# Two attention layers on one core: when the output weights are asked for, and where four key chains lie

## The chip, the cores and the metric

The kernel runs on one core of a Trainium2 chip. Times are microseconds (us) on the device, from launch to end, and lower is better. The kernel before was measured three times: 2955.73 us in the median, 2946.95 the lowest and 2957.67 the highest. A profile of one further execution shows each instruction on each engine: TensorE (PE in the profile, its weight loads PEld), VectorE (DVE), ScalarE (ACT), GpSimd (POOL), and SP, whose queue issues nearly all transfers.

## The reference

Four batches of 1024 tokens pass through two layers of cross-attention, all in float32. The context has 1024 tokens of 384 features. Layer 0 has 16 heads of 64, layer 1 has 16 heads of 32 with rotated, normalised queries and keys.

```python
# layer 0
h = layernorm(x) * gamma + beta
Q, K, V = h @ Wq, ctx @ Wk, ctx @ Wv            # 16 heads of 64
vals = (softmax(Q K^T) * 64**-0.5) @ V
x = x + vals @ Wo + bo
# layer 1
xn = x * rsqrt(mean(x * x) + eps) * norm_w
q, k, v = xn @ wq, split(ctx @ wkv)             # 16 heads of 32
q, k = rotate(q), rotate(k)                     # rotary tables cos, sin
q, k = q / max(|q|, eps), k / max(|k|, eps)
x = x + (softmax(q k^T * sqrt(32)) @ v) @ wout
```

## The kernel before, in words

**Tiles.** A batch's x is held as eight tiles of 128 tokens x 512 features. Layer 0 is worked through in eight pairs of heads (p = 0 to 7; a pair is 128 of the 1024 inner features). For each pair there are eight steps (i = 0 to 7), one for each 128 query tokens. Layer 1 follows in two halves of eight heads each.

**A step of layer 0** (`Attention0.step`). TensorE makes the scores s of both heads (line 365); VectorE takes the row maximum m (390); ScalarE computes exp into e (391); GpSimd scales e by the reciprocal of its sum (396); in the next step VectorE transposes e in blocks of 32 (399). The scores stand in two PSUM tiles, so the next step's scores wait until exp has read them. After every second step `regroup` issues sixteen transfers of 128 KB on SP (line 410), which bring the transposed blocks of e, two steps together, into place as eT: this is called a block, four in a pair. `product` (line 426) multiplies eT with the values into av; it runs in odd steps, and takes the block that is the older of two, about three steps after its regroup was asked for.

**Units.** All other work of TensorE (projections of later pairs, sums of outputs, the beginning of layer 1) is cut into units with a cost in us, and stands in a queue, `Units`. After its scores, each step takes as many units from the queue as `fill(us)` allows; `us` is all work that is still to do in layer 0, divided by the steps left. `later` is the planner's account of work that is not yet in the queue, `left` that of the values which join it at step 4 of pair 7. `made` marks how far the queue must be emptied before a pair ends. The order on every engine is the order in which the program is written out by these loops: VectorE, ScalarE, GpSimd and SP work through their instructions strictly in it.

**Output sums** (`add_units`, matmuls recorded at line 163 with the name po). For two pairs of heads together, eight sums of two units each (0.86) multiply their values with 256 rows of Wo and VectorE adds the result into a tile of x (line 293). Sums for pairs 0 and 1 stand in pairs 2 and 3, four in each; those for 2 and 3 in pairs 4 and 5; those for 4 and 5 in pairs 6 and 7; those for 6 and 7 after pair 7. `wo_load` (line 643) asks for the 256 rows, 512 KB, on SP; there are two buffers for them, shared with layer 1's output weights. The first three loads of a batch are written at the start of pairs 2, 4 and 6, the fourth at that of pair 7. In the second to fourth batch, the sums of the last half of layer 1 of the batch before (`tail`) lie in pairs 0 and 1, and the finished tiles are stored from there.

**Key chains** (`rotated_chains`). The keys of layer 1's first half are made in pairs 6 and 7, in four chains of 256 tokens. A chain has a projection (six units of 0.44, named k_p), which ends in a rotation: ScalarE squares the bank (476), VectorE multiplies it with cos and sin, adds, and sums the squares (478 to 483), GpSimd makes the norm's inverse and multiplies (485 to 489). Later its turn-over (one unit of 0.45, k_t, line 499) transposes it on TensorE and ScalarE copies it out (504). The values of the same half are four value chains of six units of 0.44 in pair 7. The wk half that the chains read is overwritten by the one for the second half, `reload`.

**Banks.** Four PSUM banks, f0 to f3, are handed out in turn by `bank` to projections, sums, turn-overs and av. A bank's next user waits until its last one has been copied or added out. While `which["from"]` is 0, which is in layer 0, a key chain's bank is remembered in `which["kept"]` and passed over each time round, until that chain's turn-over; the dictionary `kept` tells whose it is. In layer 1 three banks, f1 to f3, go round.

Of the kernel before, what the change touches and what calls it, by code (L numbers as in the profile page):

```python
# [46 lines left out]
NPAIR = INNER // P  # L47
# [61 lines left out]
def xattn_kernel(ctx: ExitStack, tc: tile.TileContext, a: dict, out: bass.AP):  # L109
    nc = tc.nc  # L110
    x, c = a["x"], a["ctx_768"]
# [12 lines left out]
    which = {"n": 0, "from": 0, "cols": 2, "kept": None}  # L124

    def bank(name):

        while True:
            which["n"] = which["n"] + 1 if which["n"] < 3 else which["from"]
            if which["n"] != which["kept"]:  # L130
                break
        return ps_f.tile([P, 512], F32, tag=f"f{which['n']}", name=name)

    def evac(dst, src):
# [315 lines left out]
    def rotated_chains(dst, src, nk, w, name, tmp):  # L450

        hd, nh = HD1 // 2, TH * FH // HD1
        tiles, kept = {}, {}

        def heads(ap):
            return ap.rearrange("p (t h d) -> p t h d", t=TH, d=HD1)

        def spread(ap):
            return ap.unsqueeze(2).to_broadcast([P, TH, FH // HD1, ap.shape[2]])

        def project(t0, i, k):
            if i == 0 and k == 0:
                tiles[t0] = [bank(f"{name}_p{t0}")]
                if which["from"] == 0:
                    which["kept"] = kept[t0] = which["n"]
            pp = tiles[t0][0]
            t = t0 + i
            lhsT = src[t // 4][:, k, (t % 4) * P : (t % 4 + 1) * P]
            matmul(pp[:, i * FH : (i + 1) * FH], lhsT, w(k), k == 0, k == nk - 1)
            if i == TH - 1 and k == nk - 1:  # L470
                rotate(t0, pp)

        def rotate(t0, pp):

            t1, t2, sq = tmp.take()
            nc.scalar.activation(sq, pp, AF.Square)
            c_, s_ = cos[:, t0 : t0 + TH, :], sin[:, t0 : t0 + TH, :]
            nc.vector.tensor_mul(heads(t1), heads(pp), spread(c_))
            nc.vector.tensor_mul(heads(t2)[:, :, :, :hd], heads(pp)[:, :, :, hd:], spread(s_[:, :, :hd]))
            nc.vector.tensor_mul(heads(t2)[:, :, :, hd:], heads(pp)[:, :, :, :hd], spread(s_[:, :, hd:]))  # L480
            nc.vector.tensor_add(t1, t1, t2)
            ss = sb.tile([P, nh], F32, tag="ss", bufs=2, name=f"{name}_s{t0}")
            nc.vector.tensor_reduce(ss, sq.rearrange("p (h d) -> p h d", d=HD1), AX.X, ALU.add)
            sm = sb.tile([P, nh], F32, tag="sm", bufs=2, name=f"{name}_m{t0}")
            nc.gpsimd.tensor_scalar_max(sm, ss, EPS_L2 * EPS_L2)
            ri = sb.tile([P, nh], F32, tag="ri", bufs=2, name=f"{name}_r{t0}")
            rsqrt(ri, sm)
            t1h = t1.rearrange("p (h d) -> p h d", d=HD1)
            nc.gpsimd.tensor_mul(t1h, t1h, ri.unsqueeze(2).to_broadcast([P, nh, HD1]))
            tiles[t0] = t1  # L490

        def turn_over(t0):
            t1 = tiles.pop(t0)
            if which["kept"] == kept.get(t0):
                which["kept"] = None
            pt = bank(f"{name}_t{t0}")
            for g in range(2):
                for i in range(TH):
                    nc.tensor.transpose(
                        pt[:, (g * TH + i) * P : (g * TH + i + 1) * P],  # L500
                        t1[:, i * FH + g * P : i * FH + (g + 1) * P],
                        ident,
                    )
            nc.scalar.copy(dst()[:, :, t0 * P : (t0 + TH) * P], pt.rearrange("p (g t) -> p g t", g=2))  # L504

        return [
            (
                [(0.44, lambda t0=t0, i=i, k=k: project(t0, i, k)) for i in range(TH) for k in range(nk)],
                [],
                [(0.45, lambda t0=t0: turn_over(t0))],  # L510
            )
            for t0 in range(0, NT, TH)
        ]
# [127 lines left out]
    def wo_load(src, i, name):  # L641
        w = sb.tile([P, 2, DQ], F32, tag="wo", bufs=2, name=name)
        nc.sync.dma_start(w, src[i * 2 * P : (i + 1) * 2 * P, :].rearrange("(n p) m -> p n m", p=P))
        return w

    def flat(lists):
        return [u for lst in lists for u in lst]
# [68 lines left out]
    for b in range(B):  # L716
# [3 lines left out]
        wo = {}  # L720
# [3 lines left out]
        for p in range(NPAIR):  # L724
            if p == 4:
                wk, wv = half_kv_load(0, 0), half_kv_load(0, 1)

            later = costs["pair"] * max(5 - p, 0) + costs["out"] * (7 - p - (b == 0 and p == 0))
            later += costs["k"] * (p < 6) + costs["v"] * (p < 7)
            other = []  # L730
            if p < 2:
                other = tail[p * len(tail) // 2 : (p + 1) * len(tail) // 2]
            elif p % 2 == 0:
                i = p // 2 - 1
                wo[i] = wo_load(a["Wo"], i, f"wo0_{b}_{i}")
                outs = add_units(
                    xt,
                    lambda n: pairs[n]["vals"],
                    lambda n, i=i: wo[i][:, n % 2, :],
                    f"po0_{b}_{i}",  # L740
                    (p - 2, p - 1),
                )
                other = flat(outs[:4])
            else:
                other = flat(outs[4:])
            if p == 6:
                kq = {}

                def begin(n, kq=kq, b=b):
                    kq[n] = qk_tile(f"{n}1_{b}_0")  # L750

                k = rotated_chains(lambda kq=kq: kq["k"], ct, NC_, lambda k, wk=wk: wk[:, k, :], f"k1_{b}_0", RowScratch())
                other = [(0.0, lambda: begin("k"))] + k[0][0] + outs[0] + k[1][0] + outs[1] + k[0][2] + outs[2] + k[2][0] + k[1][2] + outs[3]
            if p == NPAIR - 1:
                last = outs[4:]
                wo[3] = wo_load(a["Wo"], 3, f"wo0_{b}_3")
                outs = add_units(
                    xt, lambda n: pairs[n]["vals"], lambda n: wo[3][:, n % 2, :], f"po0_{b}_3", (6, 7)
                )
                xnT = []  # L760
                norms = norm_units(b, 1, xnT, lambda h: xt[4 * h : 4 * h + 4])
                v = []

                def begin_v():
                    v.extend(sb.tile([P, NT, P], F32, tag="v", bufs=3, name=f"v1_{b}_0_{g}") for g in range(2))

                vs = value_chains(v, wv, ct, f"pv1_{b}_0")
                wk1 = []
                reload = [(0.0, lambda wk1=wk1: wk1.append(half_kv_load(1, 0)))]
                other = last[0] + k[3][0] + reload + last[1] + k[2][2] + last[2] + last[3] + k[3][2]  # L770
                values = [(0.0, begin_v)] + flat(c[0] for c in vs)
            ahead = st["project"](p + 2) if p + 2 < NPAIR else []
            n = 7 * (p == 0)
            work.add(ahead[:n] + other)
            if p % 2 or other and p == 0:
                made[p + 1] = work.end()
            work.add(ahead[n:])
            if p + 2 < NPAIR:
                made[p + 2] = work.end()
            if p == 5:  # L780
                wq = []
                work.add([(0.0, lambda wq=wq: wq.append(half_q_load(0)))])
            left = costs["v"] if p == NPAIR - 1 else 0.0
            for i in range(NT):
                if b == 0 and p == 0 and i == 3:
                    work.until(begun)
                if left and i == 4:
                    work.add(values)
                    left = 0.0
                if 1 <= p <= 2 and i % 2 == 0:  # L790
                    load_x(b, xt, 4 * (p - 1) + i // 2)
                now = AV if i % 2 and len(att.blocks) == 2 else 0.0
                n = NT * (NPAIR - p) - i
                todo = work.total() + left + later + AV * ((NT * NPAIR + 1 - max(NT * p + i, 4)) // 2)
                att.step(p, i, pairs[p], max(todo / n - now, 0.0))
                if 2 <= p <= 3 and i < 2:
                    for t in range(2):
                        add_bo(xt, 4 * (p - 2) + 2 * i + t)
            if p + 1 < NPAIR:
                work.until(made[p + 1])  # L800
            else:
                work.drain()
            store_all()
# [125 lines left out]
```

## Time and profile before

| what | value |
|---|---|
| median of three runs | 2955.73 us |
| the profiled execution, launch to end | 2957.42 us |
| its span, first to last instruction | 2955.4 us |
| TensorE busy | 2865.9 us, 97% |
| VectorE busy | 2185.6 us, 74% |
| ScalarE busy | 1436.6 us, 49% |
| GpSimd busy | 935.9 us, 32% |
| transfers by SP's queue | 343.96 MB, 49.5% of the time of 16 DMA engines |
| regroup transfers (eT from e) | 2048 of 128 KB, landing in 2.4 us in the median |
| loads of Wo | 16 of 512 KB, landing in 4.4 us in the median |
| mean granted clock of TensorE | 0.992 of full speed |

In the profile's lines, `po<-wo,vals` means that po is written from wo and vals, `x16` that there are sixteen such instructions, `L163` the line of the kernel. Matmuls of float32 stand as two records each[...]. Waits are idle time of an engine, with what ended it. Times are counted from the first instruction.

### The profile page before, as it was taken

The numbers are of one execution on the slowest core, as the hardware profiler recorded it, in microseconds if no ns is written. First come the engines' busy times: TensorE is split into PE (matmuls) and PEld (weight loads), VectorE is DVE, ScalarE is ACT, GpSimd is POOL, SyncE is SP. The second block draws the span as 40 slices with busy tenths as digits, with TensorE's granted clock in tenths as the row PEclk, the third lists the DMA queues.
The fourth block names the chain that finished last, engine by engine and source line by source line (L and its number), as shares of the span: only waits on it lengthen the run. The fifth ranks groups of instructions, "written<-read, shape, count | busy, mean of one in ns | idle before, by whom it ended". The sixth has DMA issues, their size and how long they took to land.

```text
span 2955.4 us, 66614 instructions
## 1 busy us (share of the span) xinstructions
PE 2865.9 (97%) x27336; PEld 1433.0 (48%) x27336; DVE 2185.6 (74%) x2952; ACT 1436.6 (49%) x2265; POOL 935.9 (32%) x776
## 2 busy tenths in 40 slices
PE   8999999999989999999998999999999999999998
PEld 4444445555444454555544444455554444445544
DVE  5677785877767778587776777868877677786787
ACT  4444444656434443466643444346664344444664
POOL 2343353320234335332023433534102343353310
PEclk9999999999999999999999999999999999999999
DMA  5878774010487877401048787730105887763000
GB/s 141 197 180 188 169 173 104 22 36 25 105 199 176 186 163 164 104 22 36 25 115 189 179 187 170 162 94 22 36 25 126 192 182 178 172 162 85 2 2 30
DMA packets 177552, 348.86 MB, mean 118 GB/s; under 512 B 37600, under 2 KB 93152, under 8 KB 177248
## 3 DMA queue, kind: packets, MB, share of 16 engines
q1 hardware_dynamic: 175920, 343.96, 49.5%
q8 instruction: 215, 3.52, 0.5%
q14 instruction: 89, 0.73, 0.1%
q10 hardware_dynamic: 1328, 0.66, 0.1%
HBM read 67.64 MB, written 8.39 MB: 26 GB/s over the span
## 4 chain that ended last, share of the span: by engine, by line
PE 80%; DVE 10%; SPq 4%; DMA 2%; issue 2%; ACT 1%; POOL 1%; DVEq 0%; ACTq 0%
PE s L365 15%; PE av L426 13%; PE po L163 10%; PE s L577 8%; PE pqT L163 7%; PE pv L163 7%; PE av L616 6%; PE pkT L163 6%; SPq L410 4%; PE q_p L163 3%; PE av L627 2%; DVE both L593 2%; DVE m L390 2%; PE k_p L163 1%; DMA wo<-in_Wo_dram 1%
## 5 line engine op out<-in xcount | busy, mean ns | idle before, releaser
L390 DVE TENSOR_REDUCE m<-s 128x1 f32<-128x1024 f32 x512 | 603.0, 1220 | 401.6 <-PE s L365 401.6
L587 ACT ACTIVATE e<-s 128x1024 f32<-128x1024 f32 x512 | 497.1, 1023 | 313.2 <-PE s L577 304.7
L391 ACT ACTIVATE e<-s,m 128x1024 f32<-128x1024 f32 x256 | 283.4, 1112 | 502.9 <-DVE m L390 240.7
L396 POOL TENSOR_SCALAR raw<-raw,li 128x1024 f32<-128x1024 f32 x256 | 286.4, 1119 | 734.2 <-DVE li L395 725.8
L365 PE MATMUL s<-qk 64*128 64x512 f32 x2048 | 518.1, 621 | 0.7 <-ACT qk L135 0.7
L391 ACT ACTIVATE raw<-s,m 128x1024 f32<-128x1024 f32 x256 | 285.9, 1117 | 470.0 <-DVE m L390 470.0
L426 PE MATMUL av<-eT,v 128*64 128x256 f32 x4096 | 470.4, 382 | 5.3 <-DMA eT<-e 2.3
L396 POOL TENSOR_SCALAR e<-e,li 128x1024 f32<-128x1024 f32 x256 | 286.3, 1119 | 493.8 <-DMA eT<-e 239.4
L593 DVE TENSOR_TENSOR both<-e 128x512 f32<-128x512 f32 x512 | 341.9, 701 | 116.1 <-ACT e L587 88.9
L426 PEld LDWEIGHTS av<-eT,v 128*64 128x64 f32 x4096 | 287.4, 137 | 225.2 <-issue 84.5
L365 PEld LDWEIGHTS s<-qk 64*128 64x128 f32 x2048 | 180.9, 188 | 283.9 <-issue 174.3
L577 PE MATMUL s<-q,k 32*128 32x256 f32 x4096 | 306.0, 401 | 5.9 <-ACT q L504 2.7
L399 DVE STREAM_TRANSPOSE e<-e 128x1024 f32<-128x1024 f32 x256 | 310.1, 1229 | 0.2
L399 DVE STREAM_TRANSPOSE e<-raw 128x1024 f32<-128x1024 f32 x256 | 310.0, 1229 | 0.0
L163 PE MATMUL po<-wo,vals 128*64 128x512 f32 x1024 | 242.7, 608 | 26.5 <-DMA wo<-in_Wo_dram 26.5
L577 PEld LDWEIGHTS s<-q,k 32*128 32x128 f32 x4096 | 192.2, 184 | 153.0 <-ACT e L587 72.1
L163 PE MATMUL pqT<-hT,w 128*64 128x512 f32 (+1 forms) x1216 | 240.7, 595 | 2.5 <-ACT hT L247 2.5
L293 DVE TENSOR_TENSOR x<-x,po 128x512 f32<-128x512 f32 x200 | 131.7, 679 | 112.2 <-PE po L163 112.2
L163 PEld LDWEIGHTS pv<-w,cT 128*64 128x64 f32 (+1 forms) x3360 | 170.3, 132 | 41.6 <-issue 34.8
L163 PE MATMUL pv<-w,cT 128*64 128x128 f32 (+1 forms) x3360 | 184.3, 274 | 0.7 <-ACT hT L247 0.7
L163 PE MATMUL pkT<-cT,w 128*64 128x512 f32 (+1 forms) x912 | 183.1, 597 | 0.0
L597 DVE TENSOR_TENSOR both<-both 128x1024 f32<-128x1024 f32 x128 | 159.7, 1248 | 4.4
(81 smaller groups left out, 2793.1 us busy)
## 6 DMA issues: line engine op xcount, KB each, us to landing
eT<-e SPq DMA_DIRECT2D x2048, 128.0 KB, 2.4
xr<-in_x_dram SPq DMA_DIRECT2D x32, 256.0 KB, 3.6
x<-in_x_dram SPq DMA_DIRECT2D x32, 256.0 KB, 4.6
wo<-in_Wo_dram SPq DMA_DIRECT2D x16, 512.0 KB, 4.4
out_dram<-x SPq DMA_DIRECT2D x32, 256.0 KB, 2.6
w<-in_Wq_dram SPq DMA_DIRECT2D x31, 256.0 KB, 3.1
c<-in_ctx_dram SPq DMA_DIRECT2D x32, 192.0 KB, 3.9
wkv<-in_wkv_dram SPq DMA_DIRECT2D x16, 384.0 KB, 3.4
```

What stands on the lines that cost most here:

```text
L163: nc.tensor.matmul(o[rr], lhsT[:, rr], rhs, start=start, stop=stop)
L365: nc.tensor.matmul(sc[j][:, kb * 512 : (kb + 1) * 512], pr["qT"][r[j], i * P : (i + 1) * P], pr["kT"][r[j], kb * 512 : (kb + 1) * 512], st ...
L390: nc.vector.tensor_reduce(m[:, j : j + 1], sc[j], AX.X, ALU.max, negate=True)
L391: nc.scalar.activation(e[j], sc[j].rearrange("p (g s) -> p g s", g=4), AF.Exp, bias=m[:, j : j + 1], accum_out=l[:, j : j + 1])
L396: nc.gpsimd.tensor_scalar(e[j], e[j], li[:, j : j + 1], HD0**-0.5, ALU.mult, ALU.mult)
L399: self.turn = [lambda j=j: nc.vector.transpose(self.e[:, :, i % BQ * 2 + j, :], e[j]) for j in range(2)]
L426: nc.tensor.matmul(av[r[j], :W].rearrange("p (t a i) -> p t a i", t=BQ, a=4), pr["v"][:, k, r[j]], eT[:, j, :, :, k * 32 : (k + 1) * 32], ...
L577: nc.tensor.matmul(sc[j // 2][:, j % 2, c, :], kT[rr, g, k * P : (k + 1) * P], qT[rr, g, qb * WQ : (qb + 1) * WQ], start=True, stop=True,)
L587: nc.scalar.activation(e, sc[u], AF.Exp, scale=float(np.sqrt(np.float32(HD1))))
L593: nc.vector.tensor_add(self.both[:, kk, 2 * u : 2 * u + 2, :], es[u][:, :, 0, :], es[u][:, :, 1, :])
L597: nc.vector.tensor_add(self.both[:, 0], self.both[:, 0], self.both[:, kk])
L616: nc.tensor.matmul(self.av[rr, 0, :], v[g][:, 2 * kk + c, rr], es[j // 2][:, j % 2, c, :], start=first and c == 0, stop=end and c == 1,)
```

## The change

Three things are edited.

1. `wo_load` is called at the start of every odd pair, for the weights `p // 2`. Those which are used in pairs 2, 4 and 6 are thus asked for at the start of pairs 1, 3 and 5. The fourth load stays in pair 7 and is called a few lines earlier.
2. The four key chains: pair 6 has the projections of chains 0 and 1, with sums 0 and 1 between them, and the turn-over of chain 0; pair 7 has the projection of chain 2, the turn-over of chain 1 and four sums, and from step 4 on a value chain, the projection of chain 3 with the reload, the turn-over of chain 2, three value chains and the turn-over of chain 3. `later` counts the chains in two halves, and `left` is the cost of all that joins at step 4.
3. A key chain's bank is passed over once by `bank` and is then free to be handed out. The dictionary `kept` is gone.

```diff
--- before.py
+++ after.py
@@ -129,6 +129,7 @@
             which["n"] = which["n"] + 1 if which["n"] < 3 else which["from"]
             if which["n"] != which["kept"]:
                 break
+            which["kept"] = None
         return ps_f.tile([P, 512], F32, tag=f"f{which['n']}", name=name)
 
     def evac(dst, src):
@@ -450,7 +451,7 @@
     def rotated_chains(dst, src, nk, w, name, tmp):
 
         hd, nh = HD1 // 2, TH * FH // HD1
-        tiles, kept = {}, {}
+        tiles = {}
 
         def heads(ap):
             return ap.rearrange("p (t h d) -> p t h d", t=TH, d=HD1)
@@ -462,7 +463,7 @@
             if i == 0 and k == 0:
                 tiles[t0] = [bank(f"{name}_p{t0}")]
                 if which["from"] == 0:
-                    which["kept"] = kept[t0] = which["n"]
+                    which["kept"] = which["n"]
             pp = tiles[t0][0]
             t = t0 + i
             lhsT = src[t // 4][:, k, (t % 4) * P : (t % 4 + 1) * P]
@@ -491,8 +492,6 @@
 
         def turn_over(t0):
             t1 = tiles.pop(t0)
-            if which["kept"] == kept.get(t0):
-                which["kept"] = None
             pt = bank(f"{name}_t{t0}")
             for g in range(2):
                 for i in range(TH):
@@ -726,13 +725,14 @@
                 wk, wv = half_kv_load(0, 0), half_kv_load(0, 1)
 
             later = costs["pair"] * max(5 - p, 0) + costs["out"] * (7 - p - (b == 0 and p == 0))
-            later += costs["k"] * (p < 6) + costs["v"] * (p < 7)
+            later += costs["k"] * min(NPAIR - 1 - p, 2) / 2 + costs["v"] * (p < 7)
+            if p % 2:
+                wo[p // 2] = wo_load(a["Wo"], p // 2, f"wo0_{b}_{p // 2}")
             other = []
             if p < 2:
                 other = tail[p * len(tail) // 2 : (p + 1) * len(tail) // 2]
             elif p % 2 == 0:
                 i = p // 2 - 1
-                wo[i] = wo_load(a["Wo"], i, f"wo0_{b}_{i}")
                 outs = add_units(
                     xt,
                     lambda n: pairs[n]["vals"],
@@ -750,10 +750,9 @@
                     kq[n] = qk_tile(f"{n}1_{b}_0")
 
                 k = rotated_chains(lambda kq=kq: kq["k"], ct, NC_, lambda k, wk=wk: wk[:, k, :], f"k1_{b}_0", RowScratch())
-                other = [(0.0, lambda: begin("k"))] + k[0][0] + outs[0] + k[1][0] + outs[1] + k[0][2] + outs[2] + k[2][0] + k[1][2] + outs[3]
+                other = [(0.0, lambda: begin("k"))] + k[0][0] + flat(outs[:2]) + k[1][0] + k[0][2] + flat(outs[2:4])
             if p == NPAIR - 1:
                 last = outs[4:]
-                wo[3] = wo_load(a["Wo"], 3, f"wo0_{b}_3")
                 outs = add_units(
                     xt, lambda n: pairs[n]["vals"], lambda n: wo[3][:, n % 2, :], f"po0_{b}_3", (6, 7)
                 )
@@ -767,8 +766,8 @@
                 vs = value_chains(v, wv, ct, f"pv1_{b}_0")
                 wk1 = []
                 reload = [(0.0, lambda wk1=wk1: wk1.append(half_kv_load(1, 0)))]
-                other = last[0] + k[3][0] + reload + last[1] + k[2][2] + last[2] + last[3] + k[3][2]
-                values = [(0.0, begin_v)] + flat(c[0] for c in vs)
+                other = k[2][0] + k[1][2] + flat(last)
+                values = [(0.0, begin_v)] + vs[0][0] + k[3][0] + reload + k[2][2] + flat(c[0] for c in vs[1:]) + k[3][2]
             ahead = st["project"](p + 2) if p + 2 < NPAIR else []
             n = 7 * (p == 0)
             work.add(ahead[:n] + other)
@@ -780,7 +779,7 @@
             if p == 5:
                 wq = []
                 work.add([(0.0, lambda wq=wq: wq.append(half_q_load(0)))])
-            left = costs["v"] if p == NPAIR - 1 else 0.0
+            left = sum(c for c, _ in values) if p == NPAIR - 1 else 0.0
             for i in range(NT):
                 if b == 0 and p == 0 and i == 3:
                     work.until(begun)
```

## The prediction

> **What bounds the kernel now.** I read the page first: TensorE is busy for 2865.9 of 2955.4 us, so only its 89.5 us of standing still, and any work that it does slowly, can be won. Next the list of what TensorE waited for (columns: in total us, times, longest us):
>
> ```profile
> PE po L163 <- DMA wo<-in_Wo_dram: 26.5, 6, 8.7
> ...
> PE k_p L163 <- DVE x L293: 8.2, 3, 2.7
> ...
> PE av L426 <- DVE x L293: 2.1, 3, 0.7
> ```
>
> Three of its rows lie where the change works: output weights that have not landed, and PSUM banks that VectorE has not yet added into x. In order of time, the waits for weights stand at 863.6, 988.3, 1599.7, 1725.1, 2335.3 and 2456.4 us, at the start of pairs 2 and 4 of the second to fourth batch (8.39, 1.28, 8.72, 0.81, 4.86 and 2.42 us); the first batch has none. Then the chain of work, pair 2 of the second batch (start, us, what):
>
> ```profile
> 864.08 0.59 SPq L410
> ...
> 865.34 6.56 DMA wo<-in_Wo_dram
> 871.90 0.04 issue
> 871.94 5.27 PE po L163 x16
> 877.21 1.92 PE s L365 x8
> ```
>
> The load was issued at 865.34 because SP was working off sixteen regroup transfers (0.63 us each) that stand ahead of it; TensorE had wanted the weights since 863.55. Note the 5.27 us: sixteen such matmuls take 3.58 us in undisturbed places. The windows view says why (last three columns: granted clock, DMA share, GB/s):
>
> ```profile
> 871.94:877.21 5.27, 5.27 (x18) 1.49 (x18) 0.69 (x1) 0.00 (x0) 0.89 (x1) 0.69 0.93 185
> 877.21:883.59 6.38, 6.38 (x47) 3.19 (x46) 5.12 (x6) 2.68 (x5) 2.42 (x3) 1.00 0.76 163
> ```
>
> A long wait is paid twice: idle, then at a lower clock. The key chains show the same, in TensorE's timeline of pair 6:
>
> ```profile
> 1121.70 2.90 PE L365 MATMUL s<-qk 64*128 64x512 f32 x8
> ...
> 1131.66 1.97 PE L163 MATMUL k_p<-wkv,cT 128*64 128x256 f32 x8 [2.73 <-DVE x L293]
> 1133.56 3.79 PE L365 MATMUL s<-qk 64*128 64x512 f32 x8
> ```
>
> Eight score matmuls (s) normally take 1.99 us there. At 1133.56 they run at half clock, at 1121.70 they waited for ScalarE's exp, which waited for VectorE's row maximum (m). VectorE's timeline shows what held that up:
>
> ```profile
> 1115.80 0.67 DVE L478 TENSOR_TENSOR rot<-k_p,cos 128x512 f32<-128x512 f32 x1
> ...
> 1118.38 0.68 DVE L293 TENSOR_TENSOR x<-x,po 128x512 f32<-128x512 f32 x1
> 1118.97 2.35 DVE L390 TENSOR_REDUCE m<-s 128x1 f32<-128x1024 f32 x2
> ```
>
> One rotation occupies VectorE from 1115.80 to 1118.38, 2.58 us, then 0.6 us for a sum into x; the maxima of a step take 2.27 us and its transposes 2.40 us, so a step costs VectorE 4.7 us against some 6.7 us of TensorE. There is room for one rotation in two steps, not for sums bunched with it.
>
> [...] the regroup after the load at 865.34 was issued in 12.41 us and landed 4.35 us later, an undisturbed one takes 10.03 and 1.75. [...] the 2.73 us wait is a rotation that came round too early.
>
> **The change, part by part.**
>
> *Output weights one pair ahead.* The sixteen loads of Wo stay as many and as large (512 KB, one issue of about 0.5 us on SP). Those used in pairs 2, 4 and 6 are now issued at the start of pairs 1, 3 and 5, some 50 us earlier; the fourth hardly moves. Their buffer (two of them) is then free: its last readers ended in the pair before at the latest, so SP isn't held. Removed: 8.39+1.28+8.72+0.81+4.86+2.42 = 26.5 us. With them go the slow matmuls behind: 5.27, 5.67 and 5.05 us instead of 3.58 (5.2 us), and in pair 4 of the fourth batch 1.74 instead of 0.86 and 2.84 instead of 1.92 (1.8), of the second 0.2: 7.2 us.
>
> Added: each moved load now stands on SP ahead of the last regroup of the pair before (block 3), past its 16 issues and those of three more blocks, and past the x loads. SP has 1 to 3 us to spare between two regroups; the weighted-sum matmuls (av) wait for that landing with a slack, from landing to first use, of 0.2, 1.3, 1.9 and 2.8 us in pair 1 of the four batches, 2.0, 2.2, 1.4 and 2.4 in pair 3, and 1.3 to 2.5 in pair 5. In pair 1 of the second batch the SP queue is crowded just there:
>
> ```profile
> 812.34 0.35 SPq L829 DMA_DIRECT2D out_dram<-x  x1
> 812.74 0.44 SPq L279 DMA_DIRECT2D x<-in_x_dram  x1
> 813.43 10.91 SPq L410 DMA_DIRECT2D eT<-e  x16
> ```
>
> One more load costs the regroup 0.6 us of issue and about 2.5 us of transfer (512 KB at some 200 GB/s, the rate of the windows above). Bounds: nothing (the load of pair 6, which before stood in such a place at 1087.23, cost no wait) and 5.6 us (the regroup behind the load of pair 2 in the third batch: 17.4 us from first issue to landing, against 11.8). I take 3.1 us less the slack: 2.9, 1.9, 1.2 and 0.3 in pair 1, 6.3 us, lowered to 5.7 because before the third batch's regroup SP is idle for 1.3 us; in pair 3 SP has an idle gap of 1.1 to 2.3 us to hide it in, 0.3 each (1.2); in pair 5 a gap of over 3 us, nothing. Behind the waiting av are the units of its step and the next scores. Where the load has left (pair 4), two av waits of 0.65 and 0.26 us go. Net +6.0 us.
>
> *Key chains and sums.* No operation appears or vanishes; a chain has 6 units of 0.44 us, one rotation (ScalarE square, five VectorE operations, three on GpSimd of 0.25, 2.93 and 1.05 us) and one turn-over. Before, pair 6 has three projections and four sums, pair 7 one. Going through the planner's sums for both orders: before, sum 1, turn 0, sum 2 and the projection of chain 2 follow one another in step 6 of pair 6, and skipping the kept bank gives chain 2 the bank that sum 1 had two banks ago. That is the 2.73 us. After, sums 0 and 1 fall in step 4, chain 1 takes the bank of an av already copied out, av of step 5 gets sum 0's bank, turn 0 that of sum 1. VectorE ends sum 0 about 0.5 us before that av needs it; the bank is thus just free. In the second batch go 2.73, then 1.97-0.86 and 3.72-1.92 at half clock, 0.37 of av, 0.92 of scores waiting on exp, 0.71 of av waiting for a sum: 7.6 us; third 6.2, fourth 6.2, first 0.7: 20.7 us.
>
> Added: chain 1 now ends in step 6, so that rotation 1 (2.58) and sums 2 and 3 (1.2) follow that step's maxima and transposes (4.7): 8.5 us of VectorE against 6.5 of TensorE (1.92+0.43+0.59+3.58), and step 7 holds no units (5.5 us). Step 7's maxima begin 2 us late, exp ends 1.8 us after the scores of pair 7 want its banks, and they end about 2 us late, as at 1121.70 where the same lateness cost 0.92 us with one microsecond more of cover. Below this it could cost nothing (in the first batch before, the same bunch met a step of 8.3 us and cost nothing), above it 3 us with a slow clock. I take 2.0, and 0.3 for the sums of pair 7: 4 x 2.3 = 9.2 us. Chains 2 and 3 then lie alone among value chains.
>
> *The rest.* The reload of key weights moves one regroup later on SP, past pair 7's second block; it lands over 10 us before its use and its cover is the last two steps; without it 3.4 us. `later` and `left` only shift about 0.2 us a step. A bank passed over once cannot be reused before VectorE, in order, has read it; in layer 1 the three-bank sequence comes out the same, so its waits (15.4 us on both, 6.7 on rot) stay.
>
> **Sum.** Removed 26.5+7.2+20.7 = 54.4, added 6.0+9.2 = 15.2, net -39.2 us on the profiled span of 2955.4: 2916.2, and 2918.2 for that execution with the 2.0 us around it (2957.42). From the median of 2955.73, 39 less is 2916 to 2917; I say 2916.
>
> **Rivals.**
> 1. Covers hold everywhere: no late regroup, no late maximum. 2955.7-54.4 = 2901. For it: pair 6's load cost nothing before. Against: slacks of 0.2 to 1.3 us.
> 2. The wait changes its name: moved loads make av late in most of twelve places, by some 1.5 us beyond my figure, and the late maximum costs 3 us: 2916+18+3 = 2937.
> 3. Slower: the late regroup at full price. Twelve places at 5.6-1.9+1.8 us (landing delay, mean slack, slow clock) = 66 us; 2955.7-54.4+9.2+66 = 2976. It decides from 3.8 us a place (45.2/12), slower by 0.5% from 5.0. Against: the windows show DMA below full between regroups, and only two of sixteen loads saw such a delay.
> 4. The weights still come late, because a buffer is held or SP is further behind: the 33.7 us stay, 2916+34 = 2950. Against: 50 us of lead.
>
> **Chances.** Forecast 0.56, rival 1 0.17, rival 2 0.16, rival 3 0.05, rival 4 0.06. About 0.5% (14.8 us) is what a measurement of this kernel tells from no change. Faster by more, below 2941: forecast, rival 1 and nearly all of rival 2, 0.88; within 0.06; slower 0.06. The range 2901 to 2938 leaves out rivals 3, 4 and the tails; the likeliest case alone spans 2908 to 2926.
>
> **What would show it.** Right: no TensorE wait on wo, none of k_p on x; clock stretches at half gone from layer 0; new short av waits on eT in step 3 of pair 1, in the first batch some 3 us at 103 us; scores of pair 7's first step lengthened by 2 us. Wrong: av waits on eT above 20 us in all, s waits on exp in pair 6 above 15, or new waits in layer 1.

## The result, and the profile after

The changed kernel takes 2921.91 us in the median of four executions (2913.88 to 2923.36). Its ratio to the kernel before, run beside it, is 0.9892 with an interval of 0.9864 to 0.9921, so 23 to 40 us less. Measured again beside the experiments, on another chip, it was 0.9882 (0.9864 to 0.9901). The profiled execution has a span of 2912.1 us against 2955.4, 43.3 less; it is the fastest of the four, and that of before is one of the slower ones of its kernel, so the 32 to 35 us of the two ratios are what counts.

TensorE's list of waits after (columns as before; from line 130 to the key chains the line numbers stand one higher than before, behind them one lower) no longer has rows for wo and for k_p:

```profile
PE av L427 <- DMA eT<-e: 6.9, 4, 2.7
...
PE s L366 <- ACT e L392: 2.2, 3, 0.7
...
PE av L427 <- DMA out_dram<-x: 0.7, 1, 0.7
```

New at the top of layer 0's rows are weighted sums that wait for their regroup: 8.1 us in all (6.9 on eT, 0.7 behind a store, 0.5 that the list puts under issue), against 3.0 before (2.3 on eT and 0.7 in four pieces of 0.2). They lie in pair 1: 1.90 us in the first batch (0.60 of it was there before), 1.20, 0.75 and 2.74 in the second, 0.47 and 1.09 in the fourth. SP's queue at the place that the prediction showed, in the second batch:

```profile
812.43 0.57 SPq L828 DMA_DIRECT2D out_dram<-x  x1
813.05 0.45 SPq L642 DMA_DIRECT2D wo<-in_Wo_dram  x1
...
814.18 13.91 SPq L411 DMA_DIRECT2D eT<-e  x16
```

The regroup behind the load is issued in 13.91 us, three more than before. TensorE's timeline at the border of pairs 6 and 7:

```profile
1122.58 1.99 PE L366 MATMUL s<-qk 64*128 64x512 f32 x8
1124.49 3.67 PE L427 MATMUL av<-eT,v 128*64 128x256 f32 x32
1128.91 3.08 PE L366 MATMUL s<-qk 64*128 64x512 f32 x8 [0.74 <-ACT e L392]
```

The records of matmuls overlap: in the page after, the 2048 records of the scores have a mean of 0.615 us, 1260 us in all, and make 515.5 us of busy time. The first scores of pair 7 begin 0.74 us late and take 3.08 instead of 1.99 us. VectorE shows why, it works through rotation 1, then two sums, and only then the maxima of scores that had ended at 1124.5:

```profile
1122.58 0.67 DVE L479 TENSOR_TENSOR rot<-k_p,cos 128x512 f32<-128x512 f32 x1
...
1125.16 1.27 DVE L294 TENSOR_TENSOR x<-x,po 128x512 f32<-128x512 f32 x2
1126.35 2.35 DVE L391 TENSOR_REDUCE m<-s 128x1 f32<-128x1024 f32 x2
```

The trace's granted clock, a mean of 0.992 before, is 0.999: there is no stretch at half clock between the start-up and the last 10 us. That holds for this execution; the other three have means of 0.995 and 0.996, and the trace of the repeat has two stretches of 3.4 us, at 1335.8 and 2056.0 us, both in layer 1.

### The profile page after: what moved, and what is told of

It reads as the page before. It is cut to its first block, busy times and chain, and to the rows that moved or that the text cites. A ratio compares the mean times of both kernels' runs of the same rounds, so it can differ in the third digit from the quotient of the medians.

```text
span 2912.1 us, 66608 instructions
## 1 busy us (share of the span) xinstructions
PE 2852.3 (98%) x27336; PEld 1433.1 (49%) x27336; DVE 2186.5 (75%) x2952; ACT 1434.4 (49%) x2265; POOL 935.1 (32%) x776
## 3 DMA queue, kind: packets, MB, share of 16 engines
HBM read 67.64 MB, written 8.39 MB: 26 GB/s over the span
## 4 chain that ended last, share of the span: by engine, by line
PE 84%; DVE 8%; SPq 3%; DMA 2%; issue 1%; ACT 1%; POOL 1%; DVEq 0%; ACTq 0%
PE s L366 16%; PE av L427 14%; PE po L164 11%; PE s L576 8%; PE pv L164 7%; PE pqT L164 7%; PE av L615 7%; PE pkT L164 5%; PE q_p L164 3%; SPq L411 2%; PE av L626 2%; PE k_p L164 2%; DVE both L592 2%; DMA eT<-e 1%; DVE both L596 1%
## 5 line engine op out<-in xcount | busy, mean ns | idle before, releaser
L366 PE MATMUL s<-qk 64*128 64x512 f32 x2048 | 515.5, 615 | 2.9 <-ACT e L392 2.2
L164 PE MATMUL po<-wo,vals 128*64 128x512 f32 x1024 | 234.6, 596 | 0.0
```

What stands on the lines that cost most here:

```text
L164: nc.tensor.matmul(o[rr], lhsT[:, rr], rhs, start=start, stop=stop)
L366: nc.tensor.matmul(sc[j][:, kb * 512 : (kb + 1) * 512], pr["qT"][r[j], i * P : (i + 1) * P], pr["kT"][r[j], kb * 512 : (kb + 1) * 512], st ...
```

## The experiments

The theory was the prediction's sum: two parts that add up, the loads at -27.7 us (33.7 removed, 6.0 added) and the chains at -11.5 (20.7 removed, 9.2 added), the first made late by SP's order, the second by sums and rotations bunched on VectorE. The rivals were that the parts hide each other, that the wait only changes its name, that transfers are too slow to be asked for late, and that the bank rule does the work.

**The loads alone**, on the kernel before:

```diff
...
+            if p % 2:
+                wo[p // 2] = wo_load(a["Wo"], p // 2, f"wo0_{b}_{p // 2}")
...
-                wo[i] = wo_load(a["Wo"], i, f"wo0_{b}_{i}")
...
-                wo[3] = wo_load(a["Wo"], 3, f"wo0_{b}_3")
```

> Only the loads of the output weights are moved one pair ahead; the chains and the bank rule stay as before. Theory (the costs of the two parts add up): the six waits for wo (26.5 us) and the half-clock matmuls behind them (7.2) go, new av waits on eT of about 6 us net come, so about 28 us less than before, ratio 0.9905. The 2.73 us wait of k_p and the half-clock scores after it stay in three batches. Rival (the two parts hide each other, the freed time is taken up by the next late regroup): less than 15 us, ratio above 0.995.

Measured: 2934.21 us, ratio 0.9926 (0.9911 to 0.9941), some 22 us less by the ratio; the median of all 23 executions of the kernel before that stand beside this run, 2952.91 us, lies 18.7 above it. Its list of waits:

```profile
PE av L426 <- DMA eT<-e: 9.8, 4, 3.4
PE k_p L163 <- DVE x L293: 8.2, 3, 2.7
...
PE av L426 <- issue: 4.9, 6, 2.3
```

The wait for wo is gone and that of k_p stays, as the theory has it; the gain is too large for the rival and smaller than the theory's 28. Waits of av on transfers are 15.5 us here (9.8 on eT, 4.9 that the list puts under issue, 0.8 on a store), 12.5 more than before, where 6.0 were reckoned. Two of them, which end at 834.3 and 1589.6 us, are followed by 3.4 us at half clock, a price that the prediction's 6.0 us don't hold. The profile is of the slowest of the four executions (2936.90 us).

**The chains and the bank rule alone**, the changed kernel with the loads put back:

```diff
-            if p % 2:
-                wo[p // 2] = wo_load(a["Wo"], p // 2, f"wo0_{b}_{p // 2}")
...
+                wo[i] = wo_load(a["Wo"], i, f"wo0_{b}_{i}")
...
+                wo[3] = wo_load(a["Wo"], 3, f"wo0_{b}_3")
```

> Only the order of chains and sums and the bank rule are changed; the loads stay in pairs 2, 4, 6 and 7. Theory: the 2.73 us waits and their half-clock scores go (20.7 us), a late maximum before pair 7 costs about 2 us in each of three batches, so 10 to 15 us less, ratio 0.9955; the six waits for wo stay at about 26 us. Rival (the wait only changes its name, all the gain is the loads'): ratio 0.999 to 1.001.

Measured: 2942.37 us, ratio 0.9954 (0.9937 to 0.9971), 13.6 us less by the ratio and 10.5 by the medians. Its waits:

```profile
PE po L164 <- DMA wo<-in_Wo_dram: 21.4, 4, 7.1
...
PE s L366 <- ACT e L392: 2.2, 3, 0.7
```

The gain, the absence of k_p from the list and the three waits on exp are as the theory had them; the waits for wo, put at about 26 us, are 21.4. The two parts alone, 0.9926 and 0.9954, make 0.9880 multiplied, and together they measured 0.9892 and 0.9882; by the medians they make 29.2 us, and together 30.0 in the first measurement and 36.3 in the repeat. Either way they add up within the intervals.

**The bank rule alone**:

```diff
             if which["n"] != which["kept"]:
                 break
+            which["kept"] = None
...
-            if which["kept"] == kept.get(t0):
-                which["kept"] = None
```

> Only the bank rule is changed, in the kernel before. Going through the order of bank requests, chains 0 to 3 of pairs 6 and 7 get the same banks under both rules, so the theory says no change: ratio 0.998 to 1.002, and the 2.73 us waits of k_p stay. Rival (the rule is what removes the bank wait): the waits of k_p go and some 15 us with them, ratio 0.995.

Measured: 2954.09 us, ratio 1.0000 (0.9992 to 1.0008). The rule alone has no effect, so the bank wait goes only with the new order of chains and sums; whether that order would do without the new rule was not run. The run shows more: the same loads and the same waits of k_p as before, but the scores behind them ran at full speed. Its waits, and then the scores after the first k_p wait in its timeline:

```profile
PE po L164 <- DMA wo<-in_Wo_dram: 20.0, 5, 5.8
...
PE k_p L164 <- DVE x L294: 8.2, 3, 2.7
```

```profile
1128.95 1.08 PE L164 MATMUL k_p<-wkv,cT 128*64 128x256 f32 x8 [2.74 <-DVE x L294]
1129.97 1.99 PE L366 MATMUL s<-qk 64*128 64x512 f32 x8
```

In the profile before, a wait of 2.73 us at the same place was followed by scores of 3.79 us. So neither the 26.5 us for wo nor the half clock behind a 2.7 us wait is a constant of the kernel: they are of one execution.

**The loads where they were, on ScalarE's queue**, on the kernel before:

```diff
...
-                wo[i] = wo_load(a["Wo"], i, f"wo0_{b}_{i}")
+                wo[i] = wo_load(a["Wo"], i, f"wo0_{b}_{i}", nc.scalar)
```

> The kernel before, with the loads of wo for pairs 2, 4 and 6 issued at the same place of the program but on ScalarE's queue instead of SP's. Theory (the load is late because sixteen regroup issues stand ahead of it on SP, not because the transfer is slow): it is issued some 6 to 8 us earlier, the waits of 8.4, 8.7 and 4.9 us fall under 2 us each, about 20 to 28 us less than before, ratio 0.992. Rival (the 16 DMA engines are full, the load must be asked for a pair ahead): the waits stay above 5 us each and the ratio above 0.997.

Measured: 2936.53 us, ratio 0.9939 (0.9922 to 0.9955), some 18 us less by the ratio. Its waits:

```profile
PE av L426 <- DMA eT<-e: 12.0, 10, 2.2
...
PE po L163 <- DMA wo<-in_Wo_dram: 2.6, 3, 1.1
```

Without any earlier place in the program the wait for wo falls to 2.6 us, at most 1.14 each. SP's order made the weights late, not the transfer. The gain is a little below what was foreseen, since av now waits 15.4 us for transfers (12.0 on eT, 2.5 on others, 0.9 under issue).

**The changed kernel with its early loads on ScalarE's queue**:

```diff
...
             if p % 2:
-                wo[p // 2] = wo_load(a["Wo"], p // 2, f"wo0_{b}_{p // 2}")
+                eng = nc.sync if p == NPAIR - 1 else nc.scalar
+                wo[p // 2] = wo_load(a["Wo"], p // 2, f"wo0_{b}_{p // 2}", eng)
```

> The changed kernel, with the three early loads issued at the same place on ScalarE's queue, so that SP has no issue more than before the change there. Theory (the new av waits come from 512 KB that travel ahead of the regroup, 2.5 of 3.1 us, and only 0.6 us from SP's issue): av waits on eT stay between 5 and 15 us, ratio 0.988 to 0.991. Rival (SP's order is the cost): they fall to about 2 us as in the kernel before, ratio 0.986.

Measured: 2932.02 us, ratio 0.9918 (0.9901 to 0.9936), worse than both expectations. Its profile is of the slowest of the four executions, 2941.67 us where the others took 2930 to 2932. Waits of av on transfers are 22.7 us in it (16.5 on eT, 4.5 on others, 1.7 under issue). The timelines of ScalarE and SP in the second batch show where the load now falls:

```profile
812.80 0.39 ACTq L642 DMA_DIRECT2D wo<-in_Wo_dram  x1
...
799.64 21.01 SPq L411 DMA_DIRECT2D eT<-e  x24
```

ScalarE is ahead of SP; its load goes out in the middle of a regroup, one block earlier than from SP. Taking 0.6 us of issue off SP is worth less than SP's order was: there the load stands in the gap between two regroups. In all twelve places the regroup into which the load falls is issued in 13.6 to 15.7 us; the same regroups take 10.0 to 11.5 in the changed kernel. SP issues nothing in them but the regroup itself, so the lengthening of some 3 us is the price of the transfer, not of an issue on SP.

**The early loads at step 5 of the odd pairs**, in the changed kernel:

```diff
-            if p % 2:
+            if p == NPAIR - 1:
...
+                if p % 2 and p < NPAIR - 1 and i == 5:
+                    wo[p // 2] = wo_load(a["Wo"], p // 2, f"wo0_{b}_{p // 2}")
```

> The changed kernel, with the three early loads written at step 5 of pairs 1, 3 and 5 instead of at their start. Theory (a moved load costs an av wait where SP and the DMA engines are crowded, at the start of pair 1 by stores, x and pair weights): the lead is still over 20 us, so no wait for wo; av waits on eT fall from about 8 us in the changed kernel to 4 or less, time 3 to 8 us below it, ratio to before 0.987. Rival (a load costs the same wherever it stands, because every regroup has so little slack): av waits on eT stay at 8 us or more, ratio 0.989 to 0.991.

Measured: 2915.98 us, ratio 0.9860 (0.9842 to 0.9877); av waits on transfers 4.9 us (3.7 of them on eT, where 4 or less were expected), and no sum waits for wo. The run was repeated beside the changed kernel:

> The changed kernel once more, beside the next two on the same chip. Ratio to before 0.9892 as measured, between 0.987 and 0.991; the same waits of 0.74 us on exp before pair 7 in three batches, none on wo, av waits on eT between 6 and 15 us.

> The loads at step 5 of the odd pairs once more. Theory (a load is cheaper where SP is not crowded): av waits on eT at most 5 us, and 4 to 8 us less than the changed kernel on the same chip. Rival (what the first run gained was scatter from chip to chip): no more than 2 us less.

Measured: the changed kernel 2918.83 us (0.9882), av waits 7.5 us; the mid-pair loads 2915.81 us (0.9866, 0.9849 to 0.9882), av waits 6.3 us (5.0 on eT, 5 expected). On this one chip, four executions of each have means 4.5 us apart with an interval of 6.1 on either side, which does not tell them apart; over the eight of each in both measurements, from different chips, the means are 2919.8 and 2914.9 us, 4.9 apart with an interval of 3.7. The gain is in the range of the theory, and the place probably matters, but the same chip alone doesn't show it. In the repeat's SP queue the load has only one x load beside it:

```profile
856.27 0.58 SPq L642 DMA_DIRECT2D wo<-in_Wo_dram  x1
856.90 0.50 SPq L280 DMA_DIRECT2D x<-in_x_dram  x1
858.00 11.14 SPq L411 DMA_DIRECT2D eT<-e  x16
```

The regroup behind it takes 11.14 us where the one behind the load in pair 1's start took 13.91.

**A further load of 256 KB, which nothing reads, behind each early load**; it leaves the computation whole:

```diff
+                if p < NPAIR - 1:
+                    twice = sb.tile([P, DQ], F32, tag="twice", bufs=1, name=f"twice_{b}_{p}")
+                    nc.sync.dma_start(twice, a["Wo"][(p // 2) * 2 * P : (p // 2) * 2 * P + P, :])
```

> The changed kernel, with one more load of 256 KB that nothing reads, right behind each of the three early loads of a batch; it adds 12 transfers and leaves the result as it is. Theory (slack used up, each further transfer is paid in full in pairs 1 and in part in pair 3): 0.5 us of issue and some 1.2 us of transfer at each of twelve places, of which 10 to 15 us show in time, av waits on eT 15 to 25 us, ratio 0.9935. Rival (transfers are hidden anyway and the av waits are scatter): under 4 us, ratio below 0.9905.

Measured: 2927.63 us, ratio 0.9905 (0.9890 to 0.9921), av waits on transfers 14.2 us. That is some 6 us more of waits and 0.0013 to 0.0023 more of time than the changed kernel's two measurements, between the expectations: about half a microsecond for each of twelve transfers, not one. The figure is rough, since the ratios' intervals overlap and one execution's waits scatter: the run after this one has the same early loads as the changed kernel and 10.3 us of such waits. Six of the eight waits, 13.4 us, lie in pair 1; in this profile pairs 3 and 5 absorb nearly all of the transfer.

**More cover before pair 7**, in the changed kernel; 2.64 us is the cost of the six units that now stand in the queue, so that `later` no longer counts them in pair 6:

```diff
-            later += costs["k"] * min(NPAIR - 1 - p, 2) / 2 + costs["v"] * (p < 7)
+            later += costs["k"] * min(NPAIR - 1 - p, 2) / 2 + costs["v"] * (p < 7) - 2.64 * (p == 6)
...
-                other = [(0.0, lambda: begin("k"))] + k[0][0] + flat(outs[:2]) + k[1][0] + k[0][2] + flat(outs[2:4])
+                other = [(0.0, lambda: begin("k"))] + k[0][0] + flat(outs[:2]) + k[1][0] + k[0][2] + flat(outs[2:4]) + k[2][0]
...
-                other = k[2][0] + k[1][2] + flat(last)
+                other = k[1][2] + flat(last)
```

> The changed kernel, with the projection of chain 2 put in the queue one pair earlier, so that step 7 of pair 6 has about 1 us of units instead of none. Theory (the scores of pair 7 wait for exp because rotation 1 and two sums hold up VectorE for longer than TensorE has work): the cover grows by about 1 us, the 0.74 us wait before the scores goes and the lengthening of 1.1 us shrinks to under 0.7, 4 to 6 us less than the changed kernel in all, ratio to before 0.9875. Rival (the scores wait for something else, or the wait moves to the next step): the sum of both stays near 2 us per batch, ratio as the changed kernel's 0.989.

Measured: 2924.18 us, ratio 0.9896 (0.9880 to 0.9912). The wait on exp is gone, but in the same three batches av now waits 0.72 us for a sum at the border of the pairs, and the scores of step 3 of pair 7 take 0.90 us longer. The sum of the two is 1.6 us where the changed kernel has 1.8 (0.74 and 1.09): the lateness on VectorE goes where the next cover ends. This is the rival's outcome.

**Chain 1 one step earlier**, with the mid-pair loads:

```diff
-            later += costs["k"] * min(NPAIR - 1 - p, 2) / 2 + costs["v"] * (p < 7)
+            later += costs["k"] * min(NPAIR - 1 - p, 2) / 2 + costs["v"] * (p < 7) + 3.0 * (p == 6)
```

> The loads at step 5 of the odd pairs, and 3 us added to the planner's account of pair 6, so that each of its steps takes some 0.15 to 0.2 us of units more and chain 1 ends in step 5 instead of step 6: rotation 1 then stands a step ahead of sums 2 and 3. Theory (rotation 1 and two sums in one step make the maxima late): the scores of pair 7 wait less, 0.74 plus 1.09 us falls to 0.6 to 1.3 in all, with up to 0.4 us elsewhere; some 2 us less than the mid-pair loads alone. Rival (the lateness is pair 6's whole load on VectorE, whatever the order): the sum of waits stays at 1.8 us or more per batch and the time the same.

Measured: 2912.87 us, ratio 0.9860 (0.9845 to 0.9874). Rotation 1 now ends before sums 2 and 3 come; the scores of step 7 and of pair 7 in TensorE's timeline:

```profile
1118.02 3.06 PE L366 MATMUL s<-qk 64*128 64x512 f32 x8
...
1124.62 2.25 PE L366 MATMUL s<-qk 64*128 64x512 f32 x8
```

These are 1.07 and 0.26 us over 1.99, 1.3 in all instead of 1.8, at the upper end of the theory, in the second to fourth batch. In the first, whose steps fall otherwise, three delays of 1.26, 0.90 and 1.09 us stand where one of 0.90 stood. So taking the bunch apart removes 0.5 of the 1.8 us where it succeeds; the bunch is part of the cause, the rest of the lateness stays, and this edit gains nothing by it in the sum. Its av waits on transfers, 2.2 us against 5.8, make its median the lowest. Against the changed kernel on the same chip the mean is 6.8 us lower (interval 5.9), against the mid-pair loads 2.3 lower, which four executions of each don't tell apart.

## Why the prediction was right, and where its sizes were off

**The direction and the parts** were right: 2916 was forecast, 2921.9 measured, inside 2901 to 2938.

**Removed waits for wo (26.5) and half clock behind them (7.2): right in kind, too large.** They were read from one execution. Two others with the loads in the old place had 21.4 and 20.0 us of waits; the slow matmuls behind did not shrink with them. In the run with the chains alone the sixteen sums took 5.10, 6.07 and 5.36 us, in the one with the bank rule 6.60, 5.92 and 6.20, instead of 3.58, and the groups of four (one and two of them) 1.08 instead of 0.86: 6.0 and 8.4 us. So the whole term is 27.4 and 28.4 us there and not 33.7. Both of these traces are of the fastest execution of their kernel, the profile before is of one of the slower ones: at 0.992 and 2957.42 us it lay 4.5 us above the median of the 23 executions of the kernel before that stand beside the first experiments. Over these, time falls by 2.9 us for each 0.001 of mean granted clock, which is 0.001 of the span (correlation -0.80). The 5 to 6 us by which this term was too large are as much as the 4 to 7 us by which the forecast was low. Nor was the half clock behind the k_p waits a fixed cost: of the three waits of 2.73 to 2.75 us, it followed all three in the profile before and with the loads alone, two in the run with ScalarE's queue, none in that with the bank rule (the last section sets such places side by side).

**Added by the moved loads (6.0): near in the sum for the changed kernel, and that by luck; its distribution was wrong.** 8.1 and 7.5 us of av waits against 3.0 are 5.1 and 4.5 more; with the loads alone 12.5 more were measured in one profile. The step priced the regroup right behind each load. In the second batch the first wait was 1.20 and 1.00 us in two profiles (1.9 forecast), in the first batch 1.3 beyond the old one (2.9 forecast), in the third none (1.2): in the profile after 3.0 us in all where 5.7 were reckoned. But the two regroups after it, at 844 and 858 us in the second batch, came late as well, by 0.75 and 2.74, and one in the fourth by 1.09, 3.6 us more than before where nothing was reckoned. The second of them had nothing to spare before the change. It is issued behind the three loads of a later pair's weights, and in the profile before it landed 0.20, 0.88 and 0.20 us before its use in the second to fourth batch; the prediction took the slack of the first regroup alone. The same av in the second batch, before and after:

```profile
855.18 3.67 PE L426 MATMUL av<-eT,v 128*64 128x256 f32 x32 [0.20 <-issue]
...
860.56 3.67 PE L427 MATMUL av<-eT,v 128*64 128x256 f32 x32 [2.74 <-DMA eT<-e]
```

DMA engines are busy for 0.86 and 0.88 of the time in these two stretches, and for 0.73 to 0.84 in the later pairs; that the delay isn't worked off for this reason is a reading, not shown apart. Pairs 3 and 5 paid nothing, where 1.2 was reckoned.

**Removed by the order of chains and sums (20.7) and added by rotation 1 (9.2):** -11.5 forecast, 13.6 less measured (interval 8.6 to 18.6). The late maximum before pair 7 was put at 2.0 us a batch: it is 0.91 (counted from start to start; the list shows 0.74 of it) plus 1.09 in three batches, and 0.9 in the first. The further 0.3 for the sums of pair 7 came, in all four: behind the sums two groups of scores take 2.21 and 2.25 us instead of 1.99, where at most one took 2.15 before. That the bank rule changes nothing in these pairs, and that layer 1's waits stay (15.4 and 6.6 us), was right too.

**Rivals.** Covers did not hold everywhere (rival 1), the weights came in time (rival 4), and late regroups cost about half a microsecond for each of the twelve moved loads rather than the five that a slower kernel needed (rival 3). The wait did change its name (rival 2), at about the forecast's price.

## What to carry to other kernels

A transfer that was late because of its place in an issuing queue was cured here by a small step ahead (the waits for wo, 26.5 us before, were gone with the loads alone), but the place is then chosen by what stands behind it in that queue, and not in the next transfer alone: part of the delay, 0.75, 2.74 and 1.09 us in the profile after, came out two transfers further back, where there was no slack. Here the quiet middle of a pair (2915.98 us) was better than another engine's queue (2932.02 us), which ran ahead of this one and put the transfer into the middle of a stream, and probably better than the pair's crowded start (2921.91 and 2918.83 us). Where an engine in strict order has little slack (VectorE here, with 8.5 us of work against 6.5 us of TensorE's in one step by the prediction's reckoning), count its work step by step against the cover of the same step; adding cover only moved the lateness (1.6 us instead of 1.8), and taking the bunch apart reduced it in three batches (to 1.3) and raised it in the first. A profile's waits are those of one execution: before they are summed, its time and granted clock should be set against the other executions'.

## What was unexpected in the hardware

After the same idle time TensorE's clock was halved in one place and not in another. In four profiles (the kernel before, the loads alone, the bank rule alone, the loads on ScalarE's queue where they were) twelve waits of k_p lasted 2.73 to 2.75 us. Eight of them were followed by 3.4 us or more at a clock of 0.5, four by none; and after a wait of 2.74 us for a regroup in the changed kernel, from 857.8 us on, the clock stayed at 1.00. The windows view of the profile before, behind the k_p wait that ends at 1131.66 us (after the length stands TensorE's busy time, the clock is the third value from the end):

```profile
1131.66:1137.35 5.69, 5.69 (x18) 2.02 (x20) 0.55 (x1) 0.00 (x0) 1.50 (x2) 0.50 0.84 188
```

The same view of the changed kernel, with the wait at 857.8 us and what follows it:

```profile
857.80:864.00 6.20, 3.46 (x34) 2.82 (x34) 4.96 (x6) 2.30 (x4) 1.79 (x2) 1.00 1.03 187
```

It differed within one execution as well. In the run with ScalarE's queue, waits of 2.74 us ended at 1127.18 and at 2579.72 us; the first line holds the end of the one and the work behind it, the second the work behind the other:

```profile
1125.69:1129.11 3.42, 1.93 (x12) 0.98 (x14) 2.03 (x4) 0.24 (x1) 2.90 (x3) 1.00 0.41 91
...
2579.77:2583.19 3.42, 3.42 (x12) 1.57 (x14) 0.50 (x1) 0.00 (x0) 1.46 (x2) 0.50 0.83 186
```

In the profile before, the longer waits for wo, of 8.39, 8.72 and 4.86 us, were followed by mean clocks of 0.69, 0.64 and 0.72 over the sixteen sums behind them, and that of 2.42 us by 0.63 from 2458.80 to 2463.40 us. What decides between the two outcomes was not shown.
